# An LSTM that begins behind chunk 0 and twelve RNN steps, with the RNN's remaining steps beside it

## Chip, cores and metric

The kernel runs on one NeuronCore of a Trainium2 chip. The metric is the time of one execution on the device in microseconds, median of the runs. Lower is better. The names of the engines are those of the profile: PE is TensorE's matmuls, PEld its weight loads, DVE is VectorE, ACT is ScalarE, POOL is GpSimd, SP is SyncE, which issues most of the DMAs.

## What is computed

Four layers run one after another over a sequence x of shape (4, 1024, 512), all in 32-bit floats, each added to its input. `cond` has shape (4, 512).

```python
# RNN
h = cond
for t in range(1024): h = tanh(x[:, t] @ Wx0 + b0 + h @ Wh0);  y0[:, t] = h
x1 = x + y0
# SSM: a convolution over four tokens with cond as weights, then a linear scan over 64 states
conv = conv_b + sum(pad(x1)[:, k : k + 1024] * cond[k] for k in range(4))
b, c = softplus(conv @ Wp[:, :64] + bp), tanh(conv @ Wp[:, 64:] + bp);  u = x1 @ Ws + bs
for t in range(1024): s = decay * s + dt * b[:, t] * u[:, t];  y1[:, t] = c[:, t] * s
x2 = x1 + y1 @ Wo + bo
# LSTM, hidden size 512, initial h = cond, initial cell 0
i, f, o, g = gates of (x2[:, t] @ Wx2 + b2 + h @ Wh2);  cell = f * cell + i * g;  h = o * tanh(cell)
x3 = x2 + h of every t
# adapted layer: one matrix for each of the four sequences, of rank 8 beside a common one
hid = gelu(layernorm(cond) @ w1 + b1);  xa, xb = split(hid @ w2 + b2)
out = x3 + x3 @ (base + xa @ xb.T)
```

The RNN and the LSTM are recurrences over 1024 tokens, and the LSTM needs the RNN's and the SSM's result for its tokens.

## The kernel before

**Chunks and passes.** The sequence is cut into 32 chunks of 32 tokens (`NCHUNK`, `TC`). A call of `do_pass(c)` goes through the 32 tokens of LSTM chunk c. In every one of its steps the RNN of chunk c+2 also takes one step; the SSM of chunk c+1, the input projections of the LSTM for chunk c+1 (`input_mm`, `input_turn`, `input_bias`), those of the RNN for chunk c+3 (`project0`), and the adapted layer of chunk c-1 are cut into small jobs that are placed at given steps.

**Order.** The order of instructions on every engine is written by hand: the kernel is built under `tc.manual_schedule()`, so each engine runs its instructions in the order in which the program issues them. A job is a triple of step, place and function. The place is one of three in an LSTM step: "pe" (behind the step's LSTM matmuls), "gap" (before the second half's last tanh), "end" (behind the RNN's vector work).

**An LSTM step.** The hidden state is kept as three 16-bit parts (`split`), so `lstm_mm` (L362) has 96 matmuls of 12 columns. The hidden units are treated in two halves, `A` and `Bh`: each is transposed out of PSUM (L379), summed with the input projection (L384), put through the gates (L391, ACT), `products` (L395), `cell` (L400), `tanh` (L405, ACT), `h` (L408) and two `split`s (L189). The first 36 matmuls of a step need only half A's hidden state, the other 60 need half B's.

**An RNN step.** `rnn_mm` (L337) has 16 matmuls in 32-bit floats (32 in the trace), then `rnn_pre` transposes the result (L345) and adds the input projection (L346) on DVE, and `rnn_h` takes the tanh on ACT (L349). In an LSTM step, `rnn_mm` stands behind the "pe" jobs, the two others behind half B's last `split`.

**Before the first LSTM token.** The RNN runs chunk 0 (`do_pass(-2)`) and chunk 1 (`do_pass(-1)`) without the LSTM. SSM chunk 0 and the LSTM's input projections for chunk 0 are in the second of these.

**Set-up work.** A table `early` places it by pass and step: `scale_b2`, the split of the LSTM's recurrent weights into three 16-bit parts (`split_wh2`), `fold_conv` (the convolution weights times cond), the layer norm and hidden layer of the adapted layer (`adapt_norm`, `adapt_hidden`), 32 blocks of its second matmul (`adapt_w2`, L580 and its copies L585; each block of weights is a load of 512 KB into one of four buffers, and the load of block j+4 is issued on SP behind block j), a gather of the result through 32 small DMAs on POOL (`adapt_gather`, L593), its sums (`adapt_sum`), and 16 products that give the four layer matrices (`adapt_layer`, L619, L620). Sixteen of the `adapt_w2` blocks stand in the pass of RNN chunk 1, one every second step, and sixteen in steps 0 to 15 of the first LSTM pass; `base_identity` stands at its step 0 and the `adapt_layer` calls at its steps 20 to 31.

**Loop.** Chunk 0 is written out; a hardware loop of twelve unrolled passes runs twice for chunks 1 to 24; chunks 25 to 31 are written out.

Of the kernel before, what the change touches and what calls it, by code (L numbers as in the profile page):

```python
# [32 lines left out]
LOOPED = 25  # L33
# [6 lines left out]
def cond_resid_kernel(ctx: ExitStack, tc: tile.TileContext, a: dict, out: bass.AP):  # L40
# [375 lines left out]


    def ssm_jobs(c):
# [85 lines left out]
        return jobs  # L504
# [16 lines left out]
    def adapt_norm():  # L521

        nc.vector.tensor_copy(
# [3 lines left out]
        ones = xw2[1][:, 2, 0].rearrange("p t b -> p (t b)")  # L527
        nc.vector.memset(ones, 1.0 / D)
        ps = bank("pp", [P, KC, B])
        for k in range(KC):  # L530
            nc.tensor.matmul(ps[:, 0, :], ones, condT[:, k, :], start=(k == 0), stop=(k == KC - 1))
        mean = prep.tile([P, B], F32, name="mean", tag="mean")
        nc.vector.tensor_copy(mean, ps[:, 0, :])
        xc = prep.tile([P, KC, B], F32, name="xc", tag="xc")
        nc.vector.tensor_tensor(
            xc, condT, mean.unsqueeze(1).to_broadcast([P, KC, B]), ALU.subtract
        )
        sq = prep.tile([P, KC, B], F32, name="sq", tag="sq")
        nc.vector.tensor_mul(sq, xc, xc)
        ps = bank("pp", [P, KC, B])  # L540
        for k in range(KC):
            nc.tensor.matmul(ps[:, 0, :], ones, sq[:, k, :], start=(k == 0), stop=(k == KC - 1))
        rstd = prep.tile([P, B], F32, name="rstd", tag="rstd")
        nc.vector.tensor_scalar(rstd, ps[:, 0, :], EPS, None, ALU.add)
        nc.scalar.activation(rstd, rstd, AF.Sqrt)
        nc.vector.reciprocal(rstd, rstd)
        ae = prep.tile([P, KC, B], F32, name="ae", tag="ae")
# [5 lines left out]
        return ae  # L553

    def adapt_hidden():

        ae = adapt_norm()
# [14 lines left out]
    def adapt_w2(j):  # L572
# [11 lines left out]
        for t in range(4):  # L584
            nc.vector.tensor_copy(xr[CT * t : CT * t + B, half, hd, rg], ps[CT * t : CT * t + B, :])  # L585
# [48 lines left out]
    early = {(-2, 0): [scale_b2], (-2, 30): [fold_conv], (-1, 0): [adapt_hidden], (0, 0): [base_identity]}  # L634
# [15 lines left out]
    for j in range(NW2):  # L650
        half = j // (NW2 // 2)
        c, t = (-1, 2 * j + 1) if half == 0 else (0, j - NW2 // 2)
        at(c, t, lambda j=j: adapt_w2(j))
        if j % (NW2 // 2) == NW2 // 2 - 1:
            at(c, t, lambda half=half: adapt_gather(half))
    for half in range(2):
        at(-1, 2 + 2 * half, lambda half=half: adapt_bias(half))
        at(0, 19, lambda half=half: adapt_sum(half))
    for b in range(B):
        for k in range(KC):  # L660
            at(0, 20 + (b * KC + k) * 3 // 4, lambda b=b, k=k: adapt_layer(b, k))
# [30 lines left out]
    def input_jobs(c):  # L692
        jobs = []
        for n in range(TC // TG):

            ps = bank("proj2", [P, D], tag=("po", "ada")[n % 2], bufs=1)
            t = 15 + KC * n
            jobs += [(t + k, "pe", lambda n=n, k=k, ps=ps: input_mm(c, n, k, ps)) for k in range(KC)]
            jobs += [
                (t + KC - 1 + g // 2, "end", lambda n=n, g=g, ps=ps: input_turn(c, n, g, ps)) for g in (0, 2)  # L700
            ]
        jobs += [
            (23 + (KC * g + m) // 2, "end", lambda g=g, m=m: input_bias(c, 0, g, m))
            for g in range(4) for m in range(KC)
        ]
        return jobs

    def late_jobs(c):
        return [
            ((KC * g + m) // 2, "end", lambda g=g, m=m: input_bias(c, 2, g, m))  # L710
            for g in range(4) for m in range(KC)
        ]


    def do_pass(c, src=None, dst=None, lstm=True, rnn=True, ssm=True, late=True, last=False):

        jobs = []
        if dst is not None:
            jobs += adapt_jobs(c - 1, dst)
        if ssm:  # L720
            jobs += ssm_jobs(c + 1)
# [146 lines left out]
```

## Time and profile before

| | |
|---|---|
| median of three runs | 4846.65 us (4843.11, 4846.65, 14219.86) |
| the profiled execution | 4843.09 us, its span 4841.3 us |
| busy in the span | PE 4617.7 us (95%), PEld 3536.0 (73%), DVE 3830.6 (79%), ACT 1734.3 (36%), POOL 50.2 (1%) |
| mean granted TensorE clock | 0.989 |
| RNN chunk 0 alone | from 23.3 to 124.2 us of the span |
| RNN chunk 1 alone | 124.2 to 209.3 us |
| first LSTM pass | 209.3 to 383.3 us |
| second LSTM pass | 383.3 to 526.6 us |

The span runs from the first to the last instruction. A line of the profile names source line, engine, operation, output and inputs by their names in the program, shapes and count; in a timeline the two numbers ahead are start and duration in microseconds, and what stands in square brackets is the idle time of the engine before it and what ended it. "issue" there means that the engine waited for nothing that the profile shows. A 32-bit matmul counts as two in the trace. Matmuls are pipelined, so a busy PE is not a PE at its peak, and the distance between two starts tells more than the duration of one.

### The profile page before, as it was taken

The numbers are of one execution on the slowest core, as the hardware profiler recorded it, in microseconds if no ns is written. First come the engines' busy times: TensorE is split into PE (matmuls) and PEld (weight loads), VectorE is DVE, ScalarE is ACT, GpSimd is POOL, SyncE is SP. The second block draws the span as 40 slices with busy tenths as digits, with TensorE's granted clock in tenths as the row PEclk, the third lists the DMA queues.
The fourth block names the chain that finished last, engine by engine and source line by source line (L and its number), as shares of the span: only waits on it lengthen the run. The fifth ranks groups of instructions, "written<-read, shape, count | busy, mean of one in ns | idle before, by whom it ended". The sixth has DMA issues, their size and how long they took to land.

```text
span 4841.3 us, 322103 instructions
## 1 busy us (share of the span) xinstructions
PE 4617.7 (95%) x147040; PEld 3536.0 (73%) x147040; DVE 3830.6 (79%) x17908; ACT 1734.3 (36%) x8647; POOL 50.2 (1%) x94
## 2 busy tenths in 40 slices
PE   5899999999999999999999999999999999999976
PEld 3677777777777777777777777777777777777654
DVE  3588888888888888878888888888888788888776
ACT  2223333333333333333333333333333333333332
POOL 2000000000000000000000000000000000000000
PEclk6999999999999999999999999999999999999999
DMA  6310000000000000000000000000000000000000
GB/s 134 99 35 9 9 9 7 6 9 9 9 9 7 9 7 9 9 9 7 8 6 9 9 9 9 7 7 8 9 9 9 7 9 7 9 7 7 6 3 7
DMA packets 38792, 67.52 MB, mean 14 GB/s; under 512 B 9056, under 2 KB 26080, under 8 KB 36400
## 3 DMA queue, kind: packets, MB, share of 16 engines
q1 hardware_dynamic: 33488, 45.63, 3.6%
q8 instruction: 1151, 18.86, 1.6%
q10 hardware_dynamic: 1728, 1.06, 0.1%
q14 instruction: 217, 1.78, 0.1%
q0 software_dynamic: 2208, 0.19, 0.1%
HBM read 38.34 MB, written 8.39 MB: 10 GB/s over the span
## 4 chain that ended last, share of the span: by engine, by line
PE 53%; DVE 3%; issue 0%; ACT 0%; DVEq 0%
PE acc L362 34%; PE acc L337 9%; PE proj L318 5%; PE pb L292 2%; PE ada L676 1%; PE proj L292 1%; DVE tt L379 1%; DVE gc L384 1%; DVE h L189 1%; DVE h L408 0%; DVE prod L395 0%; DVE gc L400 0%; PE ssm_out L292 0%; ACT x L683 0%; DVE xw L322 0%
## 5 line engine op out<-in xcount | busy, mean ns | idle before, releaser
L362 PE MATMUL acc<-wh,h 128*12 128x256 bf16 x98304 | 2878.2, 273 | 139.2 <-DVE h L189 127.2
L362 PEld LDWEIGHTS <-h 128*12 128x12 bf16 x98304 | 2273.6, 88 | 690.2 <-DVE h L189 361.9
L379 DVE STREAM_TRANSPOSE tt<-acc 128x256 f32<-128x256 f32 x2048 | 920.5, 449 | 428.7 <-PE acc L362 311.7
L337 PEld LDWEIGHTS acc<-wh,h 128*4 128x4 f32 x32768 | 816.0, 88 | 546.0 <-issue 210.3
L337 PE MATMUL acc<-wh,h 128*4 128x128 f32 x32768 | 1114.0, 277 | 47.3 <-ACT h L349 45.1
L391 ACT ACTIVATE gc<-gc 128x32 f32<-128x32 f32 x2048 | 469.7, 229 | 1064.7 <-DVE gc L384 974.1
L384 DVE TENSOR_REDUCE gc<-tt 128x32 f32<-128x128 f32 x2048 | 778.0, 380 | 35.3
L189 DVE TENSOR_TENSOR h<-h 128x8 f32<-128x8 f32 (+1 forms) x4098 | 679.6, 166 | 104.7
L405 ACT ACTIVATE th<-gc 128x8 f32<-128x8 f32 x2048 | 427.4, 209 | 826.6 <-DVE gc L400 826.6
L349 ACT ACTIVATE h<-pre 128x16 f32<-128x16 f32 x1024 | 221.4, 216 | 1166.4 <-DVE pre L346 1166.4
L318 PE MATMUL proj<-wx,x 128*32 128x512 f32 x4096 | 528.4, 592 | 1.3 <-DVE x L494 1.3
L408 DVE SCALAR_TENSOR_TENSOR h<-gc,th 128x8 f32<-128x8 f32 x2048 | 343.0, 168 | 221.7 <-ACT th L405 204.6
L400 DVE SCALAR_TENSOR_TENSOR gc<-prod 128x8 f32<-128x8 f32 x2048 | 341.6, 167 | 35.5
L345 DVE STREAM_TRANSPOSE tt<-acc 128x128 f32<-128x128 f32 x1024 | 315.7, 308 | 64.0 <-PE acc L337 63.9
L368 ACT COPY tt<-xw 128x32 f32<-128x32 f32 x2048 | 327.9, 207 | 0.0
L395 DVE SCALAR_TENSOR_TENSOR prod<-gc 128x16 f32<-128x16 f32 x2048 | 315.2, 154 | 0.0
L330 ACT ACTIVATE xw<-xw,b2s 128x64 f32<-128x64 f32 x1024 | 293.6, 334 | 0.4
L346 DVE TENSOR_TENSOR pre<-xw,tt 128x16 f32<-128x16 f32 x1024 | 179.5, 175 | 37.8 <-DVE tt L345 0.5
L292 PE MATMUL proj<-xin,wx 128*32 128x128 f32 x4096 | 140.6, 279 | 17.9 <-DMA wh<-in_Wh_dram 16.5
L292 PE MATMUL pb<-x,wp 128*32 128x128 f32 x4096 | 138.4, 274 | 0.7 <-issue 0.4
L676 PE MATMUL ada<-layer,x 128*32 128x512 f32 x1024 | 131.5, 592 | 3.0 <-DVE x L669 3.0
L292 PEld LDWEIGHTS proj<-xin,wx 128*32 128x32 f32 x4096 | 118.6, 113 | 21.2 <-issue 18.0
(114 smaller groups left out, 1171.4 us busy)
## 6 DMA issues: line engine op xcount, KB each, us to landing
layer<-in_w2T_dram SPq DMA_DIRECT2D x32, 512.0 KB, 3.4
xin<-in_xT_dram SPq DMA_DIRECT2D x128, 64.0 KB, 2.3
out_dram<-x SPq DMA_DIRECT2D x128, 64.0 KB, 1.7
layer<-in_Wh_dram SPq DMA_DIRECT2D x16, 256.0 KB, 10.0
wx<-in_Wx_dram SPq DMA_DIRECT2D x4, 1024.0 KB, 15.0
wx<-in_Wx_dram SPq DMA_DIRECT2D x4, 256.0 KB, 6.3
wh<-in_Wh_dram ACTq DMA_DIRECT2D x4, 256.0 KB, 7.9
layer<-in_w_dram SPq DMA_DIRECT2D x4, 256.0 KB, 5.7
```

Of the source, the lines that this page charges most:

```text
L189: nc.vector.tensor_tensor(h[:, :, n], h[:, :, n - 1], upper(h[:, :, n - 1]), ALU.subtract)
L292: nc.tensor.matmul(dst[CT * j : CT * (j + 1)], columns(j), x, start=first, stop=final)
L318: nc.tensor.matmul(ps[CT * j : CT * (j + 1), :], tok, w[:, j], start=(k == 0), stop=(k == KC - 1))
L337: nc.tensor.matmul(acc0[CT * j : CT * j + B, :], h[:, k, (t - 1) % TC, :], wh0[:, k, j * P : (j + 1) * P], start=(k == 0), stop=(k == KC - 1),
L362: nc.tensor.matmul(acc2[mh][CT * j : CT * j + NP * B, :], parts, w[:, :, n0 : n0 + 2 * CT], start=(k == 0 and n == 0), stop=(k == KC - 1 a ...
L368: nc.scalar.copy(tt2[m][t % 2][:, :, :, :B], xw2[c % 2][:, :, 2 * m : 2 * m + 2, t, :])
L379: nc.vector.transpose(self.tt[:, :, :, B:].rearrange("p g c b -> p (g c) b"), acc2[self.m])
L384: nc.vector.tensor_reduce(self.gc[:, :4].rearrange("p g c b -> p (g c) b"), self.tt[:, :, :, : (1 + NP) * B].rearrange("p g c (s b) -> p ( ...
L391: nc.scalar.activation(self.gc[:, :4], self.gc[:, :4], AF.Tanh)
L400: nc.vector.scalar_tensor_tensor(self.c, self.prod[:, 1], 0.5, self.prod[:, 0], ALU.mult, ALU.add)
L405: nc.scalar.activation(self.th, self.c, AF.Tanh, scale=0.5)
L408: nc.vector.scalar_tensor_tensor(self.out[:, :, 0], self.gc[:, 2], 1.0, self.th, ALU.add, ALU.mult)
```

## The change

The RNN runs chunk 0 and the first twelve steps of chunk 1 alone; then the LSTM begins. In each of the LSTM's first twenty steps the RNN takes two steps, which brings it through chunk 1 and chunk 2's first twenty tokens; from step 20 on it takes one. Of the two, the first is issued between the 36 LSTM matmuls that need half A and the 60 that need half B, and its vector work between half A's sum and half B's transpose. The second stands where the single one stood.

Around this, work is placed elsewhere. SSM chunk 0 is squeezed into nine steps, followed by four steps with four input matmul groups each; what is not done by then (the last transpose, half of the biases) is carried into the LSTM pass as `left`. SSM chunk 1 moves ten steps later in the first LSTM pass, and its input groups come two a step. All 32 `adapt_w2` blocks stand in steps 0 to 15 of that pass, two a step, half of their copies on ACT. The layer norm is split in two and moves into RNN chunk 0, and `adapt_hidden` to step 7 of chunk 1. `base_identity` moves from step 0 to step 2, the layers to steps 21 to 30. Chunk 1's pass is written out, the loop runs over chunks 2 to 25, and chunks 26 to 31 are written out. The biases that a pass leaves over are issued ahead of the other jobs of the next pass's step; before, they came behind them.

```diff
-LOOPED = 25
+LOOPED = 26
+SHORT = 12
...
-    def ssm_jobs(c):
+    def ssm_jobs(c, slot=lambda t: t):
...
-        return jobs
+        return [(slot(t), place, f) for t, place, f in ordered(jobs)]
...
+    ones = xw2[0][:, 0, 0].rearrange("p t b -> p (t b)")
+    nc.gpsimd.memset(ones, 1.0 / D)
+    def adapt_center():
+        mean = prep.tile([P, B], F32, name="mean", tag="mean")
+        nc.vector.tensor_copy(mean, mean_over_width(condT))
+        nc.vector.tensor_tensor(xc, condT, mean.unsqueeze(1).to_broadcast([P, KC, B]), ALU.subtract)
+        nc.vector.tensor_mul(sq, xc, xc)
...
         for t in range(4):
-            nc.vector.tensor_copy(xr[CT * t : CT * t + B, half, hd, rg], ps[CT * t : CT * t + B, :])
+            copy = (nc.vector.tensor_copy, nc.scalar.copy)[t % 2]
+            copy(xr[CT * t : CT * t + B, half, hd, rg], ps[CT * t : CT * t + B, :])
...
-    early = {(-2, 0): [scale_b2], (-2, 30): [fold_conv], (-1, 0): [adapt_hidden], (0, 0): [base_identity]}
+    early = {
+        (-2, 0): [scale_b2], (-2, 24): [fold_conv], (-2, 26): [adapt_center], (-2, 28): [adapt_norm], (-1, 7): [adapt_hidden],
+        (0, 2): [base_identity],
+    }
...
-    for j in range(NW2):
-        half = j // (NW2 // 2)
-        c, t = (-1, 2 * j + 1) if half == 0 else (0, j - NW2 // 2)
-        at(c, t, lambda j=j: adapt_w2(j))
-        if j % (NW2 // 2) == NW2 // 2 - 1:
-            at(c, t, lambda half=half: adapt_gather(half))
     for half in range(2):
-        at(-1, 2 + 2 * half, lambda half=half: adapt_bias(half))
-        at(0, 19, lambda half=half: adapt_sum(half))
+        at(-1, 1 + half, lambda half=half: adapt_bias(half))
+        for j in range(NW2 // 2):
+            at(0, 8 * half + j // 2, lambda j=j + half * NW2 // 2: adapt_w2(j))
+        at(0, 8 * half + 7, lambda half=half: adapt_gather(half))
+        at(0, 20, lambda half=half: adapt_sum(half))
     for b in range(B):
         for k in range(KC):
-            at(0, 20 + (b * KC + k) * 3 // 4, lambda b=b, k=k: adapt_layer(b, k))
+            at(0, 21 + (b * KC + k) * 5 // 8, lambda b=b, k=k: adapt_layer(b, k))
...
-    def input_jobs(c):
+    def input_jobs(c, start=15, per=1, bias=(23, 32), biases=(2, 2)):
...
+            for k in range(KC):
+                t = start + (KC * n + k) // per
+                jobs.append((t, "pe", lambda n=n, k=k, ps=ps: input_mm(c, n, k, ps)))
...
+    def rnn_pass(c, steps, jobs):
+        for t in range(steps):
+            rnn_mm(c, t)
+            rnn_pre(c, t)
+            rnn_h(c, t)
+            for slot, _, f in jobs:
+                if slot == t:
+                    f()
+            for f in early.pop((c - 2, t), ()):
+                f()
+        return [(t - steps, place, f) for t, place, f in jobs if t >= steps]
...
         for t in range(TC):
+            now = rnn[t] if rnn else []
+            A, Bh = Half(c, t, 0), Half(c, t, 1)
+            lstm_mm(c, t, 0, 0)
+            lstm_mm(c, t, 0, 1, (0,))
+            for r in now[:-1]:
+                rnn_mm(*r)
+            lstm_mm(c, t, 1, 0)
+            lstm_mm(c, t, 0, 1, (1,))
+            lstm_mm(c, t, 1, 1)
             do(t, "pe")
-            if rnn:
-                rnn_mm(c + 2, t)
...
+            A.transpose()
+            A.sum()
+            for r in now[:-1]:
+                rnn_pre(*r)
+            Bh.transpose()
+            A.gates()
+            for r in now[:-1]:
+                rnn_h(*r)
+            for r in now[-1:]:
+                rnn_mm(*r)
...
+            Bh.split(2)
+            for r in now[-1:]:
+                rnn_pre(*r)
+                rnn_h(*r)
+            do(t, "end")
+            for f in early.pop((c, t), ()):
+                f()
...
-    do_pass(-2, lstm=False, ssm=False, late=False)
-    do_pass(-1, src=a["xT"][3], lstm=False, late=False)
+    rnn_pass(0, TC, project0_jobs(1, (16, 18, 20, 22)))
+    squeezed = (0, 1, 1, 2, 2, 3, 4, 4, 5, 5, 6, 6, 7, 7, 8)
+    left = rnn_pass(
+        1, SHORT,
+        ssm_jobs(0, lambda t: squeezed[t])
+        + [(3, "end", lambda: load_x(3, a["xT"][3]))]
+        + input_jobs(0, start=8, per=4, bias=(10, 13), biases=(8, 2)),
+    )
     for m in range(2):
         lstm_input(0, 0, m)
-    do_pass(0, src=a["xT"][4])
+    behind = [(1, t) for t in range(SHORT, TC)]
+    twice = len(behind)
+    behind += [(2, t) for t in range(TC)]
+    shift = twice // 2
+    left = do_pass(
+        0, left,
+        rnn=[behind[2 * t : 2 * t + 2] if t < twice else behind[twice + t : twice + t + 1] for t in range(TC)],
+        special=project0_jobs(2, (1, 3, 5, 7))
+        + ssm_jobs(1, lambda t: t + shift)
+        + [(shift + 2, "end", lambda: load_x(4, a["xT"][4]))]
+        + project0_jobs(3, (20, 21, 22, 24))
+        + input_jobs(1, start=shift + 15, per=2, bias=(29, 33), biases=(8, 2)),
+    )
```

## The prediction

> **What bounds the kernel now.** I read the page's slices first, then a table of stretches, then the order of time inside one step of three kinds: a step of the RNN alone, an LSTM step of the steady part, an LSTM step of the first pass.
>
> ```profile
> PE   5899999999999999999999999999999999999976
> PEclk6999999999999999999999999999999999999999
> ```
>
> TensorE is full from the second slice on; only the first two slices (242 us) hold idle time and a reduced clock, so only there can a reordering act. The table of stretches (length, then PE, PEld, DVE, ACT, POOL busy, granted clock, DMA share, GB/s) cuts them: chunk 0 of the RNN alone, chunk 1 alone, first LSTM pass (two parts), second pass.
>
> ```profile
> 23.30:124.20 100.90, 61.32 (x1156) 37.19 (x1148) 39.23 (x115) 24.37 (x67) 15.49 (x28) 0.58 0.54 121
> 124.20:209.30 85.10, 70.40 (x2009) 51.18 (x2004) 41.72 (x176) 18.14 (x65) 1.78 (x3) 0.92 0.31 99
> 209.30:314.90 105.60, 96.32 (x3446) 81.96 (x3436) 90.32 (x431) 33.41 (x170) 16.24 (x29) 1.00 0.24 73
> 314.90:383.30 68.40, 68.40 (x1656) 43.66 (x1648) 52.57 (x215) 19.59 (x100) 0.00 (x0) 1.00 0.01 3
> 383.30:526.60 143.30, 141.75 (x4565) 109.56 (x4568) 117.77 (x553) 53.46 (x269) 0.00 (x0) 1.00 0.03 8
> ```
>
> So the LSTM starts at 209.3, its first pass takes 174.0, a later one 143.3 (4.45 a step). A step of the RNN alone is pure latency, at half clock 2.79:
>
> ```profile
> 92.98 1.89 PE L337 MATMUL acc<-wh,h 128*4 128x128 f32 x32 [0.90 <-ACT h L349]
> 94.94 0.32 DVE L345 STREAM_TRANSPOSE tt<-acc 128x128 f32<-128x128 f32 x1 [0.18 <-PE acc L337]
> 95.50 0.22 ACT L349 ACTIVATE h<-pre 128x16 f32<-128x16 f32 x1 [1.53 <-DVE pre L346]
> 95.77 1.89 PE L337 MATMUL acc<-wh,h 128*4 128x128 f32 x32 [0.90 <-ACT h L349]
> ```
>
> The steady LSTM step is a ring of matmuls and vector work with the RNN in the gap:
>
> ```profile
> 499.79 2.80 PE L362 MATMUL acc<-wh,h 128*12 128x256 bf16 x96
> 500.62 0.31 DVE L345 STREAM_TRANSPOSE tt<-acc 128x128 f32<-128x128 f32 x1
> 501.17 0.22 ACT L349 ACTIVATE h<-pre 128x16 f32<-128x16 f32 x1 [1.07 <-DVE pre L346]
> 501.65 0.45 DVE L379 STREAM_TRANSPOSE tt<-acc 128x256 f32<-128x256 f32 x1 [0.52 <-PE acc L362]
> 502.41 1.03 PE L318 MATMUL proj<-wx,x 128*32 128x512 f32 x8
> 502.64 0.45 DVE L379 STREAM_TRANSPOSE tt<-acc 128x256 f32<-128x256 f32 x1
> 503.27 1.05 PE L337 MATMUL acc<-wh,h 128*4 128x128 f32 x32
> 504.25 2.79 PE L362 MATMUL acc<-wh,h 128*12 128x256 bf16 x96
> ```
>
> From it: a filler group holds TensorE 0.86 (502.41 to 503.27), an RNN step 0.88, 96 LSTM matmuls 2.50, so 36 of them 0.94. Half A's transpose comes 1.86 after the LSTM's first matmul, half B's 0.99 later, the next LSTM matmul 1.60 after that. The RNN's tanh ends 1.60 after the LSTM's first matmul.
>
> **The change, part by part** (us; against the profiled span 4841.3).
>
> *Chunk 0 of the RNN, before 100.9.* Same 32 latency steps, same wait for b2 after step 0. Projection 0 of chunk 1 moves from that wait and steps 10 to 12 to steps 16, 18, 20, 22: at half clock a group holds PE 1.7 (62.25 to 63.95) beside 1.45 of the step, 3.2 to 3.4 for 2.79, so about +0.5 each; three of the four cost that before too (a step of 3.41), so +0.5 net. Before, three groups in a row had raised the clock to 1.0 for 10 us (66.0 to 76.2) and made steps of 1.95 to 2.5. The layer norm moves here: two groups of 8 matmuls, 1.05 each at full clock, 1.8 at half (the like fold_conv row 119.92), each covered by the RNN's vector latency to about 1.0, so +0.8 twice; the extra table load for tanh behind Sqrt (1.28, as at 127.88) runs under the next RNN matmuls, which take 1.89; uncovered it costs 1.28. Sum +3, that is 103.9; bounds -3 (the separated groups raise the clock as well) and +8 (they never do).
>
> The Trainium skill, "TensorE: Matmul & The Clock Gate", Part 1, says a busy window of about 3.4 us releases the full rate. The record fits where groups followed each other (62.3 to 66.0); by the rule pairs of group and step, 5 us busy, might do it alone, which would make this term -1 instead of +3.
>
> *Chunk 1 alone, 32 steps in 85.1, becomes 12 steps.* The stall for adapt_hidden (10.9 between tanh 127.65 and 138.59) shrinks to its matmuls and transpose. Step by step: 2.8; two tap groups and four bias transposes with the clock still rising 5.3; the same at full clock 3.4; four steps bound by DVE's latency ops (4 reciprocals 1.1, 12 chain ops of 0.3) 2.2, 2.3, 2.3, 2.2; scan, output matmul, two x2 adds, adapt_hidden in series (0.4+0.6+1.1+0.65+0.2+1.1+1.0) 5.0; x2 adds, then four input groups 5.7; three steps of 0.88 + 4 x 0.86 = 4.3, the last less its tail. Sum 42.5, bounds 37 (adapt_hidden under cover) and 50 (half clock for half of it). The LSTM then starts at 23.3 + 103.9 + 42.5 = 169.7, 39.6 earlier.
>
> *LSTM steps 0 to 19 with two RNN steps.* In program order RNN step 1 stands behind the first 36 LSTM matmuls, and the other 60 queue behind it; its input is the tanh of RNN step 2 of the step before, which DVE reaches only after B's splits: from B's transpose 2.43 to the RNN transpose (502.64 to 505.07), 0.78 more to the tanh's end, 0.05 to TensorE: 3.27. Then 0.88, then A's transpose 0.92 later (1.86 - 0.94): 5.07. B's transpose follows after 0.99 + 0.44, the RNN transpose and add now standing between A.sum and B's transpose (505.07 to 505.51). Ring: 6.50. RNN step 2 starts 0.26 behind B's transpose, ends TensorE's part at 1.14; two w2 groups of 0.58 reach 2.30, 36 LSTM matmuls 3.24: just inside 3.27, so moved w2 work is hidden by that wait (uncovered: 16 x 1.16 = 19). Copies: two w2 groups leave 4 to DVE (0.22 each), 4 to ACT (no row; between 0.18 of L467 and 0.23 of DVE, I take 0.2, 0.8 a step, under ACT's idle half). SSM ops moved to steps 10 to 19 find 1.3 of free DVE time. 20 x 6.50 = 130; bounds 5.8 (4.45 + 0.88 + 0.44, no wait for h) and 6.9. base_identity (16 x 0.18, 3.1) overruns the free time at step 2 by 1.8.
>
> *Loads and instruction supply.* 28 loads of w2 now come two a step. Landing:
>
> ```profile
> DMA to landing us min/median/max: 3.2/3.4/4.3
> 220.32 0.61 PE L580 MATMUL pp<-layer,hid 128*4 128x64 f32 x27 [1.16 <-issue]
> ```
>
> A pair has over 12 us until used, so loads are hidden; x loads (4 x 0.42 of SP) pass ahead of one pair. The gather's 32 POOL issues (0.57 each) finish by step 17, for the sums at step 20. But the second line is a stop inside a group with no wait: ten such, 5.6 together, fall in 205 to 285 while w2 streams, against 12 in the following 4400. I price 28 loads at 0.35, two thirds on the path: 6.5; bounds 0 and 13.
>
> The Trainium skill, "Runtime: NRT & Kernel Launch", Instruction fetch mechanics, calls crossing a 16 KiB instruction block mostly hidden; by it this term would be 0. The row beside a streaming DMA queue shows otherwise, and the measurement decides.
>
> *Steps 20 to 31.* TensorE sets them, as in this pass before:
>
> ```profile
> 326.63 2.80 PE L362 MATMUL acc<-wh,h 128*12 128x256 bf16 x96
> 331.09 1.12 PE L619 MATMUL pl<-xt,xt 8*128 8x512 f32 x2
> 332.14 2.79 PE L362 MATMUL acc<-wh,h 128*12 128x256 bf16 x96
> ```
>
> One filler and one adapted layer: 5.51; a second layer or filler +0.86. With 2,2,1,2,1,2,2,1,2,1 layers in steps 21 to 30 and two input groups in 25 to 31: 4.8 + 6.7 + 6.4 + 5.5 + 6.4 + 6.4 + 7.2 + 7.2 + 6.4 + 7.2 + 6.4 + 5.6 = 76.2 (before 68.4). Bounds 72 and 81. Eight biases in steps 29 and 30 (8 x 0.29 on ACT) lie under the long TensorE step.
>
> First pass: 130 + 1.8 + 6.5 + 76.2 = 214.5, +40.5. Second pass: two input groups left for its step 0, +1.5. Steady passes: same PE and DVE order, ACT's biases before instead of behind its SSM ops in eight steps: 0, bounds -6 and +6 over 30 passes.
>
> **Sum.** -39.6 + 40.5 + 1.5 = +2.4: span 4843.7, and with 1.8 around it (4843.1 less 4841.3) 4845.5. The median shown, 4846.7, stands 3.6 above the profiled execution, and the lowest run, 4843.1, beside it; I add half of the distance: 4847.
>
> **Rivals.**
> *A, no wait for h:* the double step costs 5.8, 20 x 0.7 = 14 less: 4833. For: TensorE and DVE both have the room. Against: the tanh's place behind B's splits.
> *B, the w2 queue becomes the bound (slower):* place: steps 2 to 15; two loads a step at the slowest landing seen, 8.6, for 6.9 (ring and stops), 14 x 1.7 = +24: 4871. It decides once a load in a pair needs over 3.45. For: median 3.4. Against: that landing includes fixed latency, and the 256 KB pieces of base land 1.2 apart, 2.4 for 512 KB.
> *C, the squeezed chunk 1 runs at half clock (slower):* 16 input groups at 1.72 for 0.86, taps alike, +17: 4864. Against: TensorE would be full there, and such stretches had 1.0.
> *D, it does nothing:* RNN steps leave one stretch for another; that is nearly the forecast.
>
> **How the numbers follow.** Forecast 0.62, A 0.14, B 0.12, C 0.07, something in the steady passes 0.05. Its own terms spread about 10 either way, more upward. Range 4833 to 4866, leaving out most of B and the edge of A. About 2% (97 us) is what a measurement of this kernel can tell from no change; the whole stretch without the LSTM that could be saved is 85, and B gives 24, so only a change in every step could pass it: faster 0.01, same 0.96, slower 0.03.
>
> **What would show it.** LSTM's first matmul at 165 to 175; double steps of 6.4 to 6.9 with TensorE idle before L338, released by ACT's h; first pass 205 to 225; steady steps 4.45. Wrong if double steps fall under 6 (A), if TensorE waits for w2 loads (B), or if the clock in chunk 1's steps is near 0.5 (C).

## The result, and the profile after

The changed kernel takes 4871.20 us, median of six runs (4866.19 to 4875.85); the kernel before takes 4845.56 beside it (one of its six runs, 14219.86, is not counted in the ratio). The ratio is 1.0054, 95% interval 1.0043 to 1.0065: slower by half a per cent, inside the 2% called "the same", and 24 us above the forecast of 4847, outside its range of 4833 to 4866. The profiled execution took 4870.44, its span is 4868.7. That execution is 24.9 above the sum of 4845.5 that the prediction made for one, and the terms below add up to it.

The slices of the page show little: the clock of the second slice fell from 9 to 8, and nothing moves behind it.

```profile
PEclk6899999999999999999999999999999999999999
```

The stretches do show it (length, then PE, PEld, DVE, ACT, POOL busy with the number of instructions, granted clock, DMA share, GB/s): chunk 0 of the RNN, its twelve steps of chunk 1, the first LSTM pass in two parts, the second pass.

```profile
23.30:125.60 102.30, 61.84 (x1144) 39.16 (x1144) 39.54 (x118) 27.35 (x70) 15.62 (x29) 0.60 0.53 118
125.60:174.00 48.40, 40.32 (x732) 23.53 (x736) 17.21 (x63) 10.46 (x41) 0.00 (x0) 0.79 0.03 8
174.00:300.00 126.00, 103.23 (x3920) 91.58 (x3916) 75.47 (x374) 43.32 (x211) 10.68 (x19) 0.97 0.37 124
300.00:404.00 104.00, 95.34 (x2413) 63.36 (x2408) 73.50 (x306) 29.63 (x146) 7.32 (x14) 0.98 0.02 4
404.00:549.00 145.00, 143.44 (x4607) 109.64 (x4601) 118.10 (x554) 53.10 (x270) 0.00 (x0) 1.00 0.03 8
```

The LSTM's first matmul starts at 173.9 (before 209.4), so 35.5 are won. Its first pass, up to the last cell tanh, takes 229.9 (before 173.9), so 56.0 are lost, and 1.9 more in the second pass. In 174 to 300 TensorE is idle for 23 us of 126: this is where to look. From 220.7, 275.3 and 336.8 on, the granted clock is 0.5 for 3.4 us each; these are called half-clock windows below. The waits of TensorE in the first pass (who waited <- what ended it: us in total, times, longest):

```profile
PE pp L581 <- ACT xw L307: 8.4, 4, 2.2
PE acc L338 <- ACT h L350: 8.3, 13, 0.9
PE pl L621 <- ACT xw L307: 3.7, 3, 1.9
PE pp L581 <- issue: 3.5, 4, 2.4
PE acc L338 <- issue: 2.2, 3, 0.9
PE acc L338 <- ACT tt L369: 2.0, 1, 2.0
PE acc L363 <- issue: 1.7, 3, 0.9
```

The second line is the wait for h that the prediction's ring was built on. The first and the third are not in the prediction at all: a w2 group (L581) and an adapted layer (L621) wait for the copy that takes projection 0 out of PSUM (L307). The three lines with "issue", 7.4 together, are called stops with no named wait below. The timeline of LSTM step 1 shows how (start, duration, engine, line, idle time before and what ended it):

```profile
185.44 0.63 PE L581 MATMUL pp<-layer,hid 128*4 128x64 f32 x32
...
187.25 0.57 ACT L331 ACTIVATE xw<-xw,b2s 128x64 f32<-128x64 f32 x2
187.84 0.37 ACT L307 ACTIVATE xw<-proj,b 128x128 f32<-128x128 f32 x1
...
188.26 0.63 PE L581 MATMUL pp<-layer,hid 128*4 128x64 f32 x32 [2.19 <-ACT xw L307]
```

Projection 0, both w2 groups and the adapted layers take their PSUM from one tag ("fill") with two buffers. A step with projection 0 and two w2 groups wants three. The first w2 group runs at 185.44; the second must have the bank that projection 0 filled, and its copy stands on ScalarE at the "end" place, behind the second RNN step's tanh and two biases. Everything behind it on TensorE, the next LSTM step first, waits too.

The bare double steps (16 to 18, no set-up work) show the ring by itself: 6.20 per step, where 6.50 was predicted, with the wait for h on the first RNN step. L380 transposes half A's and half B's sums, L346 the RNN's:

```profile
302.80 0.44 DVE L380 STREAM_TRANSPOSE tt<-acc 128x256 f32<-128x256 f32 x1
...
304.40 1.16 PE L363 MATMUL acc<-wh,h 128*12 128x256 bf16 x36 [0.16 <-DVE h L190]
...
305.23 0.31 DVE L346 STREAM_TRANSPOSE tt<-acc 128x128 f32<-128x128 f32 x1
...
306.05 1.06 PE L338 MATMUL acc<-wh,h 128*4 128x128 f32 x32 [0.49 <-ACT h L350]
...
306.93 1.82 PE L363 MATMUL acc<-wh,h 128*12 128x256 bf16 x60
307.81 0.45 DVE L380 STREAM_TRANSPOSE tt<-acc 128x256 f32<-128x256 f32 x1 [1.59 <-PE acc L363]
...
309.01 0.44 DVE L380 STREAM_TRANSPOSE tt<-acc 128x256 f32<-128x256 f32 x1
```

The steps of the first pass, in the changed kernel and in the experiments that follow. A step counts from half B's cell tanh to that of the next step, and so holds what is placed at the step's end; ranges are sums, 16 to 18 the mean:

```
LSTM step            1     3     5     7  |   2  | 11 to 15 | 16 to 18 | 20 to 24 | first pass
after              8.50  8.50 10.16  8.94 | 8.15 |   40.1   |   6.20   |   35.5   |   229.9
copy in the gap    6.84  7.60  7.74  7.75 | 8.37 |   38.2   |   6.20   |   29.6   |   221.1
no w2 loads        8.50  8.50 10.16  8.50 | 8.15 |   35.1   |   6.20   |   37.0   |   223.1
no w2 at all       6.21  6.21  6.20  6.21 | 7.22 |   31.1   |   6.20   |   38.6   |   208.7
three moves        6.21  6.21  8.52  6.64 | 8.12 |   38.8   |   6.21   |   26.8   |   213.3
moves, no loads    6.20  6.21  6.31  6.22 | 6.21 |   36.9   |   6.20   |   26.8   |   202.7
```

### The profile page after: what moved, and what is told of

It is laid out like the page before. It is cut to its first block, busy times and chain, and to the rows that moved or that the text cites. A ratio compares the mean times of both kernels' runs of the same rounds, so it can differ in the third digit from the quotient of the medians.

```text
span 4868.7 us, 322086 instructions
## 1 busy us (share of the span) xinstructions
PE 4627.7 (95%) x147040; PEld 3539.5 (73%) x147040; DVE 3814.2 (78%) x17843; ACT 1742.7 (36%) x8712; POOL 50.3 (1%) x95
## 3 DMA queue, kind: packets, MB, share of 16 engines
q14 instruction: 219, 1.79, 0.1%
## 4 chain that ended last, share of the span: by engine, by line
PE 50%; DVE 3%; issue 0%; ACT 0%; DVEq 0%
PE acc L363 33%; PE acc L338 9%; PE proj L319 5%; PE pb L293 1%; PE ada L678 1%; PE proj L293 1%; DVE tt L380 1%; DVE gc L385 1%; DVE h L190 1%; DVE h L409 0%; DVE prod L396 0%; DVE gc L401 0%; PE ssm_out L293 0%; ACT x L685 0%; DVE xw L323 0%
## 5 line engine op out<-in xcount | busy, mean ns | idle before, releaser
L380 DVE STREAM_TRANSPOSE tt<-acc 128x256 f32<-128x256 f32 x2048 | 920.5, 449 | 469.3 <-PE acc L363 353.6
L401 DVE SCALAR_TENSOR_TENSOR gc<-prod 128x8 f32<-128x8 f32 x2048 | 341.9, 167 | 35.5
L346 DVE STREAM_TRANSPOSE tt<-acc 128x128 f32<-128x128 f32 x1024 | 315.9, 308 | 38.7 <-PE acc L338 37.9
L369 ACT COPY tt<-xw 128x32 f32<-128x32 f32 x2048 | 327.9, 207 | 0.0
L319 PEld LDWEIGHTS proj<-wx,x 128*32 128x32 f32 x4096 | 118.2, 110 | 20.5 <-issue 15.1
```

The costliest lines, as they stand in the source:

```text
L319: nc.tensor.matmul(ps[CT * j : CT * (j + 1), :], tok, w[:, j], start=(k == 0), stop=(k == KC - 1))
L369: nc.scalar.copy(tt2[m][t % 2][:, :, :, :B], xw2[c % 2][:, :, 2 * m : 2 * m + 2, t, :])
L380: nc.vector.transpose(self.tt[:, :, :, B:].rearrange("p g c b -> p (g c) b"), acc2[self.m])
L401: nc.vector.scalar_tensor_tensor(self.c, self.prod[:, 1], 0.5, self.prod[:, 0], ALU.mult, ALU.add)
```

## The experiments

They ran in four groups, each on one chip beside runs of the kernel before, which took 4835.70, 4850.33, 4832.36 and 4834.99 in the four. So ratios and stretches are compared, not times of different groups. In the expectations the stretch "RNN step 31 to the LSTM's first matmul" (51.1) begins one RNN step early, and so does the end of "chunk 0": a table load in the tanh's line had been counted as a tanh. Below, the stretch begins at the tanh of step 31 (48.3 in the changed kernel), and chunk 0 goes from the first RNN tanh to that one (100.4; before the change 97.5).

**The copy of projection 0 in the gap.**

```diff
-            jobs += [(t, "pe", mm), (t, "end", end)]
+            jobs += [(t, "pe", mm), (t, "gap", end)]   # in the first pass
```

> Only the place of eight copies changes: in the LSTM's first pass ScalarE empties the PSUM bank of each group of projection 0 in the gap of its own step, ahead of the second RNN step's tanh and the biases, not behind them. Theory (a shared PSUM bank: the second w2 group and the adapted layer wait for that copy, 8.4 us in 4 and 3.7 in 3, and two of the three 3.4 us windows at half clock follow these waits): the waits fall under 0.5 each, steps 1, 3, 5 and 7 from 8.5, 8.5, 10.2, 8.9 to about 6.7, the first pass from 229.9 to 217 to 220, the run about 4859. Rival (the pair of w2 loads is what the steps wait for): the waits only change their name, first pass 229 or more, run 4871. Rival (instruction supply): the same, unchanged.

Measured: ratio 1.0038 (1.0024 to 1.0052), first pass 221.1, against 229.9. Both waits for L307 are gone. What stands in the list in their place:

```profile
PE acc L338 <- ACT h L350: 7.9, 13, 0.7
PE acc L363 <- issue: 5.4, 6, 2.1
PE acc L338 <- issue: 5.2, 8, 1.1
PE pp L581 <- issue: 3.0, 4, 1.9
```

The shared bank is shown: only the place of eight copies changed. But of 12.1 us of waits and the half-clock windows behind them only 8.8 came back, 5.8 of it from step 20 on and 3.0 ahead of it: steps 1, 3, 5, 7 fell by 6.2 but stayed above the 6.7 expected, and the steps between them rose. The stops with no named wait rose from 7.4 to 13.6: TensorE now runs into them where it had stood waiting.

**The streamed loads left out.**

```diff
         if j + W2_BUFS < NW2:
-            load_w2(j + W2_BUFS)
+            w2[j + W2_BUFS] = w2[j]
```

> The 28 streamed w2 loads of the first pass are left out (the first four blocks are used again, so the adapted layer is another one); matmuls, copies and gathers stay. Rival B of the prediction (the loads' queue is the bound): the steps 2 to 15 fall to about 6.9, first pass 24 shorter, 206, run 4847. Theory of the shared bank: the waits behind projection 0's copy stay at 8.4 and 3.7; at most the stops with no wait (7.4 us in 11, and a stop of 2.0 that the trace puts down to ScalarE) go, with the half-clock window behind the longest: first pass 219 to 230, run 4860 to 4871. If the stops stay as well, loads and stops have nothing to do with each other.

Measured: ratio 1.0036 (1.0024 to 1.0049), first pass 223.1, 6.8 shorter. The bank waits stay:

```profile
...
PE pp L581 <- ACT xw L307: 8.8, 4, 2.2
PE pl L621 <- ACT xw L307: 3.7, 3, 1.9
PE acc L338 <- issue: 1.9, 4, 0.6
```

So rival B, whose price of 24 happened to give the measured 4871, is not what happened: with no loads at all the first pass would have had to fall to 206, and in the changed kernel no wait ends on a w2 load. What the loads cost are the stops, with the half-clock window behind the longest of them (from 275.3). Steps 0 to 19, beside which the loads run, take 140.9 for 149.2, so 8.3; the whole pass shows only 6.8, as a longer half-clock window (6.8 us from 327.4) happens to stand in its steps 20 to 24. The 2.0 put down to ScalarE's L369 went with the loads; it was such a stop (its place is 512 TensorE instructions behind the stop at 240.04, and further below this distance turns out to be the mark of them).

**The w2 groups left out whole.**

```diff
-            at(0, 8 * half + j // 2, lambda j=j + half * NW2 // 2: adapt_w2(j))
+            pass
```

> The w2 groups are left out whole (matmuls, copies and the streamed loads; the gather moves what lies there, so the adapted layer is another one); projection 0 stays where it is. As the prediction had it (w2 hidden by the wait for h, only 6.5 of stops): first pass 223, double steps 6.2 with and without. Theory: w2 costs what the steps show over the bare 6.2, 8.4 of bank waits, 9.4 of stops, two half-clock windows of 1.7 and some 0.4 in each clean step: double steps 6.2 to 6.5, first pass 203 to 208 (the adapted layers' bank waits of 3.7 stay), run 4845 to 4850.

Measured: ratio 1.0000 (0.9990 to 1.0010), first pass 208.7. Every double step is 6.20 to 6.23 except step 2 (7.22, base_identity): projection 0 in steps 1, 3, 5, 7 and the SSM's taps in 11 to 14 cost nothing by themselves, they fit under the ring's idle time. The w2 work as a whole costs 24.5 in steps 0 to 19 (124.7 for 149.2) and 21.2 in the pass, not the 6.5 of the prediction. The adapted layers' bank waits stayed, with two half-clock stretches beside them (step 24 at 10.6), which is why the pass is 0.7 above what was expected.

**adapt_hidden earlier in the RNN's twelve steps.**

```diff
-(-1, 7): [adapt_hidden]
+(-1, 4): [adapt_hidden]
-    squeezed = (0, 1, 1, 2, 2, 3, 4, 4, 5, 5, 6, 6, 7, 7, 8)
+    squeezed = (0, 1, 1, 2, 2, 3, 4, 4, 5, 5, 6, 6, 7, 7, 7)
```

> In the twelve steps of the RNN alone, adapt_hidden moves from step 7 to step 4 and the last two x2 adds from step 8 to step 7. Theory (steps 8 and 9, 7.9 and 7.4 for 5.0 and 5.7, are a chain in series: scan, output matmul, x2 adds, memset and matmul of adapt_hidden, RNN step 8, and only behind its transpose the last x2 adds that the input groups wait for): adapt_hidden (0.97 + 1.9) and the wait of 1.2 leave the chain, RNN steps 31 to the LSTM's first matmul 51.1 falls to 45 to 47, run about 4866. Rival (the half clock from 145.6 alone makes these steps long): the chain is as long as before, 50 to 51, as TensorE is still idle there.

Measured: ratio 1.0046 (1.0029 to 1.0062), stretch 48.1 against 48.3: my theory fell, and the number is the rival's (50.8 in the counting of the expectation). Steps 8 and 9 fell from 7.94 and 7.37 to 5.20 and 5.86, as the theory had it, but step 5, behind adapt_hidden's new place, rose by 3.8, from 1.96 to 5.75. A half-clock window (139.2 to 142.6) stands in that step; how much of the 3.8 is the clock's was not separated.

**The second RNN step's tanh ahead of B's h.**

```diff
             Bh.tanh()
+            if len(now) == 2:
+                rnn_pre(*now[1]); rnn_h(*now[1])
             Bh.h()
...
-            for r in now[-1:]:
+            for r in now if len(now) == 1 else ():
                 rnn_pre(*r); rnn_h(*r)
```

> In the double steps, the second RNN step's transpose, add and tanh go ahead of half B's h and splits, into VectorE's 0.27 of idle time while ScalarE makes B's tanh. The prediction's ring: the first RNN step of the next LSTM step waits for this tanh (0.49 in the bare steps 16 to 18). If the place of the tanh sets the ring, the bare steps fall from 6.20 to 5.7 or 5.8; a w2 step has only 0.2 of that wait left and falls by 0.2, so the first pass gets 3 to 6 shorter, 224 to 227 after 229.9. Rival (B's h and splits are what the ring waits for, they come 0.2 later now): bare steps stay at 6.2 or rise to 6.4, first pass 230 to 234.

Measured: ratio 1.0042 (1.0029 to 1.0056), first pass 230.3, no gain. Yet the ring moved: the bare steps went from 6.20 to 5.56, and the wait of the first RNN step is gone.

```profile
305.11 1.16 PE L363 MATMUL acc<-wh,h 128*12 128x256 bf16 x36 [0.16 <-DVE h L190]
306.10 1.06 PE L338 MATMUL acc<-wh,h 128*4 128x128 f32 x32
```

So the tanh's place sets the ring, as the prediction argued against its rival A. The w2 steps gained nothing on the whole: bank waits fell to 4.7 and stops with no named wait rose to 13.2 (and 2.0 more of them put down to L369).

**Three moves.** Projection 0 of both chunks and base_identity go where nothing else wants the bank or VectorE.

```diff
-        special=project0_jobs(2, (1, 3, 5, 7))
+    chunk2 = project0_jobs(2, (4, 5, 6, 7))        # in the RNN's twelve steps
...
-        + project0_jobs(3, (20, 21, 22, 24))
+        + project0_jobs(3, (16, 17, 18, 19))
...
-        (0, 2): [base_identity],
+        (-1, 9): [base_identity],
```

> Three pieces of set-up work leave the steps in which they collide: projection 0 of chunk 2 from LSTM steps 1, 3, 5, 7 to steps 4 to 7 of the RNN alone (TensorE idles there 0.9 to 1.5 a step), projection 0 of chunk 3 from steps 20 to 24 to the bare steps 16 to 19, base_identity from LSTM step 2 to step 9 of the RNN alone (under 4.3 of input groups). Theory (shared bank, and what follows from it): steps 1, 3, 5, 7 fall by 2 or more each, 20 to 24 by 6 together and by 3.4 of moved groups, step 2 by 1.8, steps 16 to 19 rise by at most 0.2; some of the stops that lay under the bank waits come out. First pass 208 to 217, RNN steps 31 to the LSTM's first matmul 48 to 52, run 1.000 to 1.003 of the kernel before. Rival (the groups cost their 0.86 wherever they stand): first pass shorter by 10 only, the RNN alone 3 to 7 longer, run 1.004.

Measured: ratio 1.0009 (0.9999 to 1.0018), first pass 213.3, RNN stretch 44.2 (47.0 in the counting of the expectation, 1 under its range). This takes back nearly all of the loss. Steps 16 to 18 with a projection in them stay at 6.21, and steps 20 to 24 fall by 8.7. In the RNN stretch, steps 8 and 9 are 5.42 and 5.72, at clock 1.0, where the changed kernel had 7.94 and 7.37. The stops are 13.1 now, no bank wait is left.

**Both edits together.**

> The edits of the last two runs in one kernel. If both act on their own: first pass 3 to 6 under that with the moves alone, run 0.999 to 1.002 of the kernel before. If the ring is not set by the tanh's place: as with the moves alone, or 2 to 4 longer.

Measured: ratio 1.0013 (1.0004 to 1.0022), first pass 216.2. The bare steps fell to 5.57, and the time went into stops again: 18.3 for 13.1.

**The moves without the loads.**

> The three moves, without the 28 streamed w2 loads (the first four blocks are used again, so the adapted layer is another one). Theory: beside the moves alone only the stops with no named wait go, 7 to 13 us of them; the double steps with w2 are then 6.2 to 6.6, the first pass 200 to 204. Rival (the w2 groups and their copies cost something by themselves, uncovered): double steps near 7, first pass 208 or more.

Measured: ratio 0.9992 (0.9983 to 1.0001), first pass 202.7, 10.6 under the moves alone. Steps 1 to 10 are 6.2 to 6.6, two w2 groups included: "w2 is hidden by the wait for h" was right for them. Beside the run without loads and without the moves this gives the price of the bank with hardly a stop in the way: steps 1, 3, 5 and 7 take 24.9 together without projection 0 and 35.7 with it, a half-clock window in step 5 included. Steps 11 to 15 are not hidden (36.9 for 31.1 without w2): in them two w2 groups and a group of taps come together. Of the 5.8, 4.2 are stops with no named wait, even without the loads; TensorE gets 69 instructions a us there.

**Loads in short rows.**

```diff
-        nc.sync.dma_start(out=w, in_=a["w2T"][j])
+        for q in range(0, 2 * D, D // 2):
+            nc.sync.dma_start(out=w[:, q : q + D // 2], in_=a["w2T"][j][:, q : q + D // 2])
```

> The three moves, with each w2 load of 512 KB cut into four of 128 KB, 1 KB in a row for 4 KB. The stops with no named wait come to 13.2 us in the first pass with the moves alone, and to 4.6 without the streamed loads. Theory (the instruction supply waits behind the long rows of the loads on the same DMA engines): shorter rows let it through, the stops fall under 8, first pass from 213 to 205 to 209, run 1.000 or less of the kernel before. Rival (the bytes count, not the rows): stops of 11 or more, first pass 211 to 216, run 1.001.

Measured: ratio 1.0010 (1.0000 to 1.0020), first pass 211.7, stops 12.4. The rival holds: shorter rows do not let the instructions through. But the trace shows what the stops are. Stretches of this kernel (steps 2 to 10), and of the moves without loads:

```profile
191.10:254.70 63.60, 52.15 (x2038) 44.32 (x2024) 40.38 (x201) 24.52 (x123) 9.06 (x16) 1.00 0.50 154
```

```profile
185.60:242.50 56.90, 51.11 (x2032) 44.13 (x2019) 40.21 (x201) 24.47 (x123) 9.07 (x16) 1.00 0.03 6
```

The first two brackets count TensorE's matmuls and weight loads. With loads streaming it gets 4062 of them in 63.6 us, 64 a us; without, 4051 in 56.9, 71 a us. From step 11 on the stops end at 255.18, 258.92, 263.48, 266.94, 271.22, 274.69, 279.25 and 282.98. The count of TensorE's instructions in the trace from one stop to the next gives 256 each time. Ahead of step 11 it gives 256, 512 or 1024, and in the first pass of every kernel here that has stops it gives multiples of 256, to one instruction (its few semaphore instructions are counted with the matmuls and weight loads). The DMA view of this run lists a queue for instructions (packets, MB, share of 16 engines):

```profile
q8 instruction: 1151, 18.86, 1.6%
```

Its packets have 16 KB each, and 48 of them fall in this first pass, as many as TensorE has blocks of 256 there. Of the 207 stops in the first passes of the fifteen kernels that have any, each ends 1.2 to 1.6 us behind the end of such a packet (258.92 behind 257.52, 263.48 behind 262.00). So such a stop is a wait for the next block of instructions. The packet takes no longer beside the loads (1.04 in steps 1 to 10 of the moves, 1.14 without the loads); it starts later, 1.74 us after TensorE has begun the block before, against 0.85. The Trainium skill, "Runtime: NRT & Kernel Launch", Instruction fetch mechanics, says that instructions are fetched in blocks of 256; the distance of the stops agrees. It also says that the fetch is hidden because the engine dispatches more slowly than the blocks come; here, beside a streaming load, the runs show 12 to 13 us that are not.

**Fewer instructions beside the same loads.**

```diff
-            for t in range(4):      # column tiles of a w2 group, and their copies
+            for t in range(1):
```

> The three moves, with all 32 w2 loads at their places, but of the four column tiles of each w2 group only the first is multiplied and copied (the other three are left out, so the adapted layer is another one): 352 TensorE instructions in a step (matmuls and weight loads) for 448, 416 for 512 where the taps stand. Theory (with loads streaming, TensorE gets only some 64 instructions a us: 448 in 7.0 and 512 in 8.0 with short loads, both 64; so the group's instructions are what the stops hold up): 352 in 6.2 is 57, under that, so steps 1 to 10 go at 6.2 to 6.4 with hardly a stop, first pass 200 to 204. Rival (each load stops TensorE some 0.35 by itself, whatever it works at): the same loads give the same stops of 10 or more, steps of 6.6 to 7.5, first pass 208 to 212.

Measured: ratio 0.9983 (0.9973 to 0.9993), first pass 204.3, stops 7.7 with all 32 loads in place. In steps 1 to 10, beside some 20 of the 28 streamed loads, three stops are left (1.59, 0.50, 0.76), where the moves alone have ten; so a load does not cost a stop by itself, and the prediction's price per load is the wrong kind of price. But in steps 11 to 15 four stops (4.8 together) remain, at 56 instructions a us on the mean. A single rate of 64 does not cover that. These four end 1.2 to 1.6 behind an instruction packet as well; the packet ahead of the longest (1.61, over at 254.32) had started at 251.95, 3.0 after the block before was begun. What makes a packet start late beside a load stays open.

**Spare matmuls in chunk 0.** The last question came from rival C and from the half-clock steps: what does half clock cost the RNN alone?

```diff
             rnn_mm(c, t)
+            if spare is not None:                  # chunk 0 only, a bank that nothing reads
+                nc.tensor.matmul(spare, xin[0][:, 0].rearrange("p t b -> p (t b)"), wx0[:, 0, :], start=True, stop=True)
```

> The three moves, and one matmul of 128x128 by 128x512 into a spare bank in each of the 32 steps of chunk 0, behind the RNN's own matmuls; nothing reads it. It asks what half clock costs the RNN alone (steps of 2.79 in which TensorE works 1.89; 2.0 where the clock was 1.0). Theory (the granted clock follows how full TensorE is): with 0.86 more per step at full clock TensorE is some 87% busy, the clock rises to 1.0 a few us after the wait for b2 and stays, steps fall to 2.0 to 2.2, chunk 0 from 96 to 100 to 74 to 82, run 0.995 to 0.998 of the kernel before. Rival (the clock does not rise): the matmul costs 1.7 in a step that has 0.9 free, steps of 3.5, chunk 0 at 115 to 120, run 1.004 or more.

Measured, with the moves: ratio 1.0001 (0.9991 to 1.0010). The clock does rise to 1.0 at 46.8 and stays there for 205 us, and chunk 0 falls to 92.2 (100.4 in the changed kernel, 103.4 with the moves). Two steps in the trace are 2.04 apart, where they took 2.79:

```profile
84.06 1.06 PE L338 MATMUL acc<-wh,h 128*4 128x128 f32 x32
85.05 1.13 PE L724 MATMUL spare<-wx,xin 128*128 128x512 f32 x2
86.10 1.06 PE L338 MATMUL acc<-wh,h 128*4 128x128 f32 x32
```

That the whole is less than expected is in good part the splits' doing: they stand on VectorE ahead of the RNN's transpose, and the steps that hold two of them take 2.52 where those without take 1.95. Most of the rest is in the steps that hold a projection or the layer norm, up to 4.2 each. In the variant with all edits, further below, the spare matmul starts at 60.29, behind the RNN's own, and the RNN's transpose starts only at 61.00, behind a split:

```profile
60.29 1.12 PE L725 MATMUL spare<-wx,xin 128*128 128x512 f32 x2
60.40 0.69 DVE L279 SCALAR_TENSOR_TENSOR xw<-layer,wh 128x512 f32<-128x512 f32 x1
61.00 0.31 DVE L347 STREAM_TRANSPOSE tt<-acc 128x128 f32<-128x128 f32 x1
```

**The scaling of b2 at step 10 as well.**

> As with the spare matmuls, and the scaling of b2, which makes VectorE wait for b2's last piece ahead of the second RNN step's transpose (15.4 us between the first two tanhs), goes from step 0 to step 10. If the RNN has what it needs by then, that wait goes and chunk 0 gets 12 to 15 shorter than with the spare matmuls alone, 60 to 68, run 0.992 to 0.995. Rival: the weights' splits, which wait for their own loads, take its place and hold the RNN up at step 4, and only 3 to 6 are left.

Measured: ratio 0.9977 (0.9967 to 0.9986), chunk 0 at 81.5, 10.7 less: the first two tanhs are now 2.3 apart for 14.4. The wait goes, but 60 to 68 and a ratio of 0.992 to 0.995 were expected: the steps stay at 2.6 on the mean (79.2 over thirty), with the splits between them.

**All of it.**

> All of it: the three moves, the spare matmuls, the scaling of b2 at step 10, loads of 128 KB, and the second RNN step's tanh ahead of B's h. If the short loads halve the stops, the tanh's place pays now (bare steps of 5.56 for 6.20): first pass 198 to 206, run 0.989 to 0.992 of the kernel before. If the stops stay, the time that the tanh's place frees goes to them: first pass 213 to 218, run as with the spare matmuls and b2.

Measured: ratio 0.9965 (0.9953 to 0.9978), the fastest of all these kernels. The first pass is 210.0, between the two ranges; the stops are 13.7, so the short loads did not halve them. The bare steps are 5.57; the w2 steps still go at the pace of the supply, 63 instructions a us in steps 2 to 10.

**The kernel before with the two edits of chunk 0.**

> The kernel before the change, with the spare matmuls in chunk 0 and the scaling of b2 at step 10, nothing else. These two act in chunk 0 alone, which both kernels have. If they are independent of the change: chunk 0 from 97 to 80 to 84, the rest as before, run 0.995 to 0.998 of the kernel before; the best variant so far (0.9965) then owes all of its gain to them and nothing to the change. If the change, repaired, adds something: this one stays above 0.998.

Measured: ratio 0.9969 (0.9958 to 0.9981), chunk 0 at 79.7, the LSTM's passes as before (173.4, 143.1). So the gain of the best variant belongs to chunk 0. The change itself, with every collision that was found taken out, is worth nothing that these runs can tell: 0.9965 and 0.9969 lie well inside each other's intervals, which reach some 6 us to either side.

## Why the prediction was wrong

**What held.** Chunk 0: 103.9 predicted, 102.3 measured. Part of that is luck: the terms named there add up to 2.1 and not to the 3 of the sum, and in the kernels here that share this code chunk 0 ends anywhere from 122.9 to 128.8. Beside the separated groups the clock did rise to 1.0, from 84.2 to 101.2, which the sum had only as its lower bound. The LSTM's start was to be at 165 to 175 and is at 173.9. The ring of the double step is limited by the second RNN step's tanh behind B's splits, and this wait was summed rightly (3.27; 302.80 to 306.05 is 3.25). The ring's 6.50 measures 6.20, under the 6.4 to 6.9 that were to show it, which gives back 6.0 in twenty steps. The term that was mis-sized is another one: from A's transpose to B's, 0.99 + 0.44 was summed and 1.20 is measured (307.81 to 309.01), so that about half of the RNN's transpose and add costs nothing there. A smaller slip goes the same way: 96 LSTM matmuls hold TensorE 2.62 by the prediction's own lines (499.79 to 502.41), not 2.50, so A's transpose comes 0.88 behind the RNN step and not 0.92. The loads never make a group wait. The stops, priced at 6.5, cost 8.3. The second pass: +1.5 predicted, +1.9 measured. The steady passes: from the second pass's end to that of the 31st, 3.3 more than before, and 1.7 in the last pass and its tail; both lie inside the plus or minus 6 given. Four kernels of one group with the same steady code differ by 4.8 there, so no cause is named.

**What failed: "moved w2 work is hidden by that wait".** The sentence weighed TensorE's time alone. It asked whether two w2 groups and 36 matmuls end before h comes, and left out the PSUM bank that a group needs. Steps 1, 3, 5 and 7 have projection 0, a third taker of two banks, and lose 11.3 over the bare step (36.1 less 4 times 6.20), with a half-clock window of 3.4 us from 220.7 on, behind the wait in step 5. Without the loads, and so without most of the stops, it is 10.9 (35.7 less 24.8). The experiment with the copies in the gap shows the mechanism, the one without w2 shows that projection 0 has no cost there otherwise. The prediction names projection 0 in chunk 0 alone and says nowhere that its other eight groups stand in steps 1, 3, 5, 7 and 20 to 24. So the first pass, which was to take 205 to 225, takes 229.9.

**The same bank once more, in steps 20 to 31.** Predicted 76.2, measured 80.7: the three waits of L621 are 3.7, with another half-clock window at 336.8.

**Three into one idle time.** In steps 11 to 15 the SSM's taps were checked against VectorE's free time only. On TensorE taps alone are free, two w2 groups alone nearly so, both together are not: without loads these five steps take 35.1 in the changed kernel for 31.0 of bare ones, so 4.1. About half of it, 2.2, are stops, waits for instructions that a step with 512 of them brings even without loads; that term the prediction did not have at all.

**The RNN's twelve steps.** Predicted 42.5, measured 48.3. Steps 8 and 9 take 7.94 and 7.37 where 5.0 and 5.7 were summed. These lines show it:

```profile
148.19 1.93 PE L293 MATMUL ssm_out<-w,wo 64*32 64x128 f32 x32 [1.49 <-DVE w L486]
...
151.09 1.89 PE L564 MATMUL pp<-layer,ae 128*4 128x128 f32 x32 [0.97 <-PE ssm_out L293]
...
152.75 1.94 PE L338 MATMUL acc<-wh,h 128*4 128x128 f32 x32
```

Three groups take 1.9 each that take 0.9 to 1.1 at full clock; the granted clock was 0.5 from 145.6 to 159.3. How much of it falls on the chain is chance: the same code in this stretch gave 7.94 and 7.3 to 7.4 in three kernels, but 6.72 and 5.72 with the copy in the gap, where one window of 3.4 fell on it. At full clock, with projection 0 in the steps ahead, the two took 5.42 and 5.72, 4.2 less; of the eight kernels with the three moves, four have step 8 at 5.4 and the other four, with one window of 3.4 on it, at 6.7 to 7.1. This is rival C, in two steps rather than in the input groups where it was looked for; its argument against, "TensorE would be full there", was true of the groups and not of the chain ahead of them. The rest of the miss is 1.3 in the steps ahead of them (21.8 for 20.5).

The sum: -1.6 for chunk 0, +5.8 for the twelve steps, +15.4 for the first pass (229.9 less 214.5; of it -6.0 ring, +10.9 bank, +4.1 steps 11 to 15, +1.8 stops beside the loads, +4.5 steps 20 to 31, which leaves 0.1), +0.4 for the second, +5.0 behind it: 25.0, to a tenth the 24.9 above the forecast's own sum. Rival B's 4871 is met to a fifth of a us, by a mechanism that it does not name; a time that fits is no evidence for a cause.

## What to carry to other kernels

When work is said to hide under a wait, list every resource that it takes there, not the engine's time alone: its PSUM buffer, who frees it, and where on that engine's queue the freeing copy stands. Count the groups that share a buffer tag in one step; the third taker of two buffers waits for the slowest evacuation of the step. And take a wait away only after asking what is next: here each us won from the bank or from the ring went for a good part into stops that had been lying under it.

## What was not expected of the hardware

- Stops of TensorE with no named wait are not a price per load but waits for its own instructions: they stand multiples of 256 TensorE instructions apart, and all 207 of them end 1.2 to 1.6 us behind a 16 KB packet of the instruction queue. Without streaming loads TensorE got 71 instructions a us over nine steps with next to no stop; with them it got 62 to 64, and the stops came to 12 to 19 us in one pass of the kernels with the three moves.
- An idle time of some 2 us in TensorE can cost a further window of 3.4 us at half clock. In the changed kernel three such windows followed waits of 1.8, 2.4 and 1.9; waits of 2.2 at three other places had none. The Trainium skill, "TensorE: Matmul & The Clock Gate", Part 1, says that the window runs freely and does not start with the work; waits of the same length with and without a window fit that, and so does the trace, where the changes of the clock stand whole multiples of 3.41 us apart. How idle such a stretch must be does not come out of these runs: in the changed kernel 333.35 to 336.75, in which TensorE worked 1.79, was followed by half clock, and 234.4 to 237.8, in which it worked 1.48, was not.
- One matmul of some 1 us that nothing reads, in every step of chunk 0, kept the clock at 1.0 for the rest of chunk 0 and the RNN's twelve steps (46.8 to 159.9), also behind the last of them: chunk 1's first two steps took 2.11 and 1.95, against 2.85 and 2.78 in the changed kernel. In the two variants of the changed kernel with b2's scaling at step 10 as well, one half-clock window of 3.4 fell into the twelve steps (from 128.8 and 128.9).
